# Layer 0's y tiles in three long runs between inner products, instead of eight short ones

## The chip, the cores and the metric

The kernel runs on one core of one Trainium2 chip. A core has a matrix engine (TensorE, PE in the profile, with its weight loads as PEld), a vector engine (VectorE, DVE), an activation engine (ScalarE, ACT), a general engine (GpSimd, POOL) and a queue engine (SyncE, SP) that issues most of the DMAs. Each engine takes its instructions in the order of its own list, and waits on semaphores for the others. The metric is the device time of one execution, in microseconds; the value given for a kernel is the median of its runs.

## The reference

Four layers of a graph network work on `x` (8 batches x 2048 nodes x 64 features) with one adjacency matrix `adj` (2048 x 2048). Each layer adds its result to `x` and normalises over the features. The change lies in layer 0, and in the first part of layer 1:

```python
    w = jnp.einsum('nd,dkio->nkio', embedding, weight)      # d = 16, k = 3
    b = jnp.einsum('nd,do->no', embedding, bias)
    As = [jnp.eye(N, dtype=x.dtype)]
    As.append(A)
    As.append(2.0 * (A @ As[-1]) - As[-2])
    A_stack = jnp.stack(As, 0)
    x_g = jnp.einsum('knm,bmc->bnkc', A_stack, x)
    out = jnp.einsum('bnki,nkio->bno', x_g, w)
    return out + b
    ...
    x = _layernorm(x + _L0_gnn_ref(x, adj, L0_gnn_embedding, L0_gnn_weight, L0_gnn_bias), axis=-1)
    x = _layernorm(x + _L1_gnn_ref(x, 0, L1_gnn_net_params, adj), axis=-1)
```

Layer 1 multiplies by `adj` and by a 64 x 64 matrix, with a relu, twice. Layers 2 and 3 multiply by `adj` and by small matrices too. All is in float32. `T1` is `adj @ x`, and `T2` is `adj @ T1`; the kernel folds the factor 2 and the subtraction into the weights `wn`.

## The kernel before

**Products with the adjacency.** `x` and its successors lie in SBUF as `xy`: 128 nodes in the partitions, 16 node tiles, two slots, and 512 columns (8 batches x 64 features). A product with `adj` is made in `product`, by a scheme of seven products instead of eight, at two levels. The outer level cuts nodes and columns into halves, so the result has four *quarters* (node half, column half), and makes seven inner products, in the order A11, S1, A12, S2, S4, S3, A22. Each of them (`inner`) makes seven block products (`mul`, L229). A block product loads one 1 MB tile `a` of the adjacency, or of a prepared sum of its blocks, with one DMA on SyncE (`load`, L192 or L194), and makes four matmuls of 128 x 128 weights with 512 columns (L244, or L237 in other products). The tiles `a` come from a ring of four buffers, so the loads run up to four block products ahead. From layer 1 on there are three buffers more (`ring2`, opened in `to_late`), in the memory that layer 0's last stage had used.

The block products of an inner product are made in the order `pa` (block 0), `pb` (5), `pa` (1), `pb` (6), `pc` (4), `pb` (3), `pc` (7). These are three banks of PSUM in use, but the pool `p_mm` has two: `pc` gets the one that `pa` leaves, and the next `pa` gets the one that `pb` leaves. ScalarE copies `pa` to `p1` (L259), and VectorE does the rest (L207): the operand sums `t1` to `t4`, the sums `u2` and `u3`, which have to read `pb` before the next block product adds into it, and the adds that finish a block and free its bank.

**Where y comes from.** The last product of layer 0 gives T2, feature by node, in tiles `C`. `hand_over` gives each finished 128 x 512 block as a job to the *pump*: `feature0` (L811 to L848). A job fetches its tiles of `xT` and `tT` (x and T1, feature by node) with two DMAs on SyncE, one job ahead, from two buffers each. It then has four node tiles, with two y tiles each: six matmuls in pairs, each pair being one call on the lower and one on the upper 64 rows (L829), into 128 x 1024 values. VectorE adds the first y tile into `xy`, weighted with the embedding, in eight instructions (L837). ScalarE weights the second in eight (L841), and GpSimd sums these in a tree and adds them to `xy` (L846, L848). A job has 48 matmul calls. There are sixteen jobs, four to a quarter.

After each pair of neighbouring jobs follows a layer norm (`layernorm`, L375 on), put off by `defer` for four steps of the pump: its square on GpSimd (L396, one buffer), then, four steps later, VectorE's reduction (L402, kept in program order), small operations, ScalarE's square root (L407) and the scaling (L412). A quarter has two of them.

**What sets the order.** The program's order is that of the pump: after every block product, `mul` calls `pump.step(rate)`, and `step` takes the number of steps from the first job, when `batch` steps are owed. With `rate=4` and `batch=16` that is sixteen steps, two jobs of 96 matmul calls in all, after every four block products. Steps that have no job count half for deferred norms. `pass_mark` at the start of the next product takes all jobs up to the mark (set after S4, so the quarters (0,0) and (0,1)), and `flush(False)` takes the norms that the next product needs. The quarters come in the order (0,0), (0,1), (1,1), (1,0). A scheduler then orders the instructions of each engine by priority as far as dependencies, buffers and `keep_in_program_order` allow it: so single y matmuls that need only x can be moved ahead, into earlier inner products.

In layer 1, `product` is called with the first two inner products, A11 and S1, ahead of `pump.drain()`, which ends layer 0's jobs, and of `to_late`, which gives back its pools.

Of the kernel before, what the change touches and what calls it, by code (L numbers as in the profile page):

```python
# [29 lines left out]
class Pump:  # L30


    def __init__(self):
        self.jobs = []
        self.later = []
        self.rate = 1
        self.gate = None
        self.owed = 0
        self.batch = 1

    def add(self, gen):
        self.jobs.append(gen)
# [22 lines left out]
    def tick(self, idle=False):  # L65
        for job in list(self.later):

            job[0] -= 0.5 if idle and job[4] else 1
            if job[0] <= 0:
                job[0], job[4] = job[1], False  # L70
                if next(job[2], "done") == "done":
                    self.later.remove(job)

    def step(self, n=1, now=False):
        self.owed += n
        if self.jobs and self.owed < self.batch and not now:
            return
        n, self.owed = int(self.owed), self.owed - int(self.owed)
        while n > 0 and (self.jobs or self.later):
            try:  # L80
                idle = not self.jobs
                if not idle:
                    next(self.jobs[0])
                n -= 1
                self.tick(idle)
            except StopIteration:
                self.jobs.pop(0)
# [8 lines left out]
def kernel(  # L96
# [18 lines left out]
    nc = tc.nc  # L115
# [7 lines left out]
    NP = B // 2  # L123
# [70 lines left out]
            nc.sync.dma_start(a, comb[q][s].rearrange("p (n m c) -> p n m c", n=TG, m=TG))  # L194
        return a

    def product(src, feature, between=None, rate=1, own=None, pin=False, batch=1, onto_slot=None):

# [9 lines left out]
        def new_t():  # L210
            return sums.tile([P, NT // 2, 4 * F], F32, tag="T", name="T", bufs=3)
# [4 lines left out]
        def inner(q, b, finish, early=None):  # L216


            b11, b12, b21, b22 = (
                b[:, hm * TG : (hm + 1) * TG, ts(hc, 2 * F)] for hm in range(2) for hc in range(2)  # L220
            )

            def new():
                return sums.tile([P, TG, 2 * F], F32, tag="t", name="t", bufs=5)

            t1 = add(new(), b12, b11, ALU.subtract)
            t2 = add(new(), b22, t1, ALU.subtract)
            t3 = add(new(), b22, b12, ALU.subtract)
            t4 = add(new(), b21, t2, ALU.subtract)  # L229

            def mul(ps, s, xb, start, stop=True):
                a = load(q, s)
                if onto_slot is not None:

                    for k in range(TG):
                        for m in range(TG):
                            nc.tensor.matmul(  # L237
                                ps[:, ts(k, P)], a[:, k, m, :], xb[:, m, :],
                                start=(start and k == m == 0), stop=(m == TG - 1), skip_group_check=True,
                            )  # L240
                    pump.step(pump.rate)
                    return
                for m in range(TG):
                    nc.tensor.matmul(  # L244
                        ps, xb[:, m, :], a[:, :, m, :], start=(start and m == 0),
                        stop=(m == TG - 1), skip_group_check=True,
                    )
                pump.step(pump.rate)

            def bank(n):  # L250
                nonlocal banks
                banks += 1
                pool = p_mm if p_mm2 is None or banks % 3 else p_mm2
                return pool.tile([P, GW], F32, tag="mm", name=f"mm{n}")

            pa, pb = bank("a"), bank("b")
            mul(pa, 0, b11, True)
            p1 = sums.tile([P, GW], F32, tag="p1", name="p1")
            nc.scalar.copy(p1, pa)  # L259
            if early is not None:  # L260
                early(2, p1)
            mul(pb, 5, t2, True)
            u2 = add(sums.tile([P, GW], F32, tag="u2", name="u2"), pb, p1)
            if early is not None:
                early(1, u2)
            mul(pa, 1, b21, False)
            finish(0, pa, None)
            mul(pb, 6, t3, False)
            u3 = add(sums.tile([P, GW], F32, tag="u3", name="u3"), pb, p1)
            if early is not None:  # L270
                early(3, u3)
            pc = bank("c")
            mul(pc, 4, t1, True)
            finish(3, pc, u3)
            mul(pb, 3, t4, False)
            finish(2, pb, p1)
            mul(pc, 7, b22, False)
            finish(1, pc, u2)

        def fresh(c):  # L280
            def finish(blk, ps, plus):
                if plus is None:
                    nc.scalar.copy(c[:, blk, :], ps)
                else:
                    add(c[:, blk, :], ps, plus)
            return finish,
# [42 lines left out]
        if pin:  # L329
            tc.keep_in_program_order(sub)  # L330
        inner(A11, b11, *fresh(u))
        inner(S1, t1, *fresh(v))
        pump.drain()
        pump.rate, pump.batch = rate, batch
        if between is not None:
            between()
        t2 = new_t()
# [3 lines left out]
        prior(0, 0)  # L341
        c = new_c()
        inner(A12, b21, *onto(c, u, (0, 0)))
        t3 = new_t()
        sub = nc.vector.tensor_tensor(t3, b22, b12, ALU.subtract)
        if pin:
# [3 lines left out]
        prior(1, 0)  # L350
        c = new_c()
        inner(S2, t2, *onto(u, u, then=lambda blk: add(c[:, blk], u[:, blk], v[:, blk])))
        inner(S4, b22, *onto(c, c, (0, 1)))
        pump.mark()
        prior(1, 1)

# [4 lines left out]
            hand_over(v, 1, 1, blk)  # L361

        inner(S3, t3, *onto(u, u, then=last))
        inner(A22, t4, *onto(u, u, (1, 0)))

    def to_nodes(dst, pool, tiles, p, hT):
# [72 lines left out]
    if True:  # L439
# [353 lines left out]
        if True:  # L793
            p_y = first.enter_context(tc.tile_pool(name="p_y", bufs=3, space=PSUM))
            l0y = first.enter_context(tc.tile_pool(name="l0y", bufs=1))
            e_sb = l0y.tile([P, NT, D], F32, tag="e_sb", name="e_sb")
            nc.gpsimd.dma_start(e_sb, emb)


            order = [  # L800
                (2 * ih + k // 2, 2 * ch + k % 2)
                for ih, ch in ((0, 0), (0, 1), (1, 1), (1, 0)) for k in DONE
            ]
            fetched = {}

            def fetch(k):
                if k < len(order):
                    i, p = order[k]
                    fetched[i, p] = [l0y.tile([P, GW], F32, tag=n, name=n, bufs=2) for n in ("xT", "tT")]
                    for tile_, src in zip(fetched[i, p], (xT, t1T)):  # L810
                        nc.sync.dma_start(tile_, src[p][:, ts(i, GW)])  # L811

            def feature0(g, p, hT):
                if (g, p) == order[0]:
                    fetch(0)
                fetch(order.index((g, p)) + 1)
                terms = fetched.pop((g, p)) + [hT]
                for k in range(TG):
                    t = g * TG + k
                    acc = xy[:, t, 0, ts(p, 2 * F)].rearrange("p (b f) -> p b f", f=F)  # L820


                    s = l0y.tile([P, DH, 2, F], F32, tag="s", name="s", bufs=2)
                    for h in range(2):
                        y = p_y.tile([P, 2, DH * F], F32, tag="y", name="y")
                        for n in range(3):
                            for b in range(2):
                                half = slice(b * F, (b + 1) * F)
                                nc.tensor.matmul(  # L829
                                    y[:, b, :], terms[n][half, ts(k, P)],  # L830
                                    wn[half, n, h * DH : (h + 1) * DH, :],
                                    start=(n == 0), stop=(n == 2),
                                )
                        for d in range(DH):
                            e = e_sb[:, t, h * DH + d : h * DH + d + 1]
                            if h == 0:
                                nc.vector.scalar_tensor_tensor(  # L837
                                    acc, y[:, :, ts(d, F)], e, acc, ALU.mult, ALU.add
                                )
                            else:  # L840
                                nc.scalar.activation(s[:, d], y[:, :, ts(d, F)], AF.Copy, scale=e)  # L841
                        if h == 0:
                            yield
                    n = DH // 2
                    while n:
                        nc.gpsimd.tensor_tensor(s[:, :n], s[:, :n], s[:, n : 2 * n], ALU.add)  # L846
                        n //= 2
                    nc.gpsimd.tensor_tensor(acc, acc, s[:, 0], ALU.add)  # L848
                    yield

            product(1, then(feature0, 0, gap=4, pool_sq=True), rate=4, batch=16)


    late = p_z = None
# [127 lines left out]
```

## Time and profile before

| what | value |
|---|---|
| median of three runs | 1682.71 us (1682.04 to 1684.85) |
| the profiled execution, its own time | 1684.56 us |
| its span, first to last instruction | 1682.8 us |
| mean granted clock of TensorE | 0.997 |
| instructions in the profile | 20633 |
| HBM read and written | 339.85 MB, 50.33 MB |
| y matmuls (L829), union of their time | about 395 us (133.1 + 131.3 + 131.2) |
| first and last y matmul | 220.7 and 744.0 us from the span's start |

The profile is that of one execution. *Busy* is the time in which at least one instruction of an engine was running. TensorE's matmuls overlap, and their ends are modelled, so distances between starts say more than durations. A row of the timeline gives the start, the time to the end of the last instruction that it merges, engine, line of the kernel, operation, output and inputs, their shape, and the number merged; in brackets stands the idle time ahead of it and what is taken to have ended it. Where several semaphores are waited for, that is the one that came last by the profile, and not always the true one.

### The profile page before, as it was taken

The numbers are of one execution on the slowest core, as the hardware profiler recorded it, in microseconds if no ns is written. First come the engines' busy times: TensorE is split into PE (matmuls) and PEld (weight loads), VectorE is DVE, ScalarE is ACT, GpSimd is POOL, SyncE is SP. The second block draws the span as 40 slices with busy tenths as digits, with TensorE's granted clock in tenths as the row PEclk, the third lists the DMA queues.
The fourth block names the chain that finished last, engine by engine and source line by source line (L and its number), as shares of the span: only waits on it lengthen the run. The fifth ranks groups of instructions, "written<-read, shape, count | busy, mean of one in ns | idle before, by whom it ended". The sixth has DMA issues, their size and how long they took to land.

```text
span 1682.8 us, 20633 instructions
## 1 busy us (share of the span) xinstructions
PE 1666.6 (99%) x8176; PEld 1045.7 (62%) x8176; DVE 946.1 (56%) x1690; ACT 265.9 (16%) x763; POOL 250.3 (15%) x332
## 2 busy tenths in 40 slices
PE   9999999999999999999999999999999999999997
PEld 4688844444444444444454455589998455579997
DVE  5587893555546556454533365863568344543666
ACT  0100000421332332330011011220001011100001
POOL 1121200542435544450000000000000000000000
PEclk9999999999999999999999999999999999999999
DMA  9998888135233223309877877657888866678894
GB/s 341 351 359 309 306 312 305 42 113 189 87 125 113 68 71 126 113 34 366 307 268 269 307 252 262 224 209 273 293 292 299 305 217 230 230 266 296 315 311 155
DMA packets 82288, 391.53 MB, mean 233 GB/s; under 512 B 8880, under 2 KB 25264, under 8 KB 42640
## 3 DMA queue, kind: packets, MB, share of 16 engines
q1 hardware_dynamic: 69504, 346.78, 58.3%
q0 software_dynamic: 11248, 42.08, 6.5%
q10 hardware_dynamic: 1440, 1.35, 0.3%
q8 instruction: 65, 1.06, 0.2%
q14 instruction: 31, 0.25, 0.0%
HBM read 339.85 MB, written 50.33 MB: 232 GB/s over the span
## 4 chain that ended last, share of the span: by engine, by line
PE 96%; DVE 3%; POOL 0%; ACT 0%; issue 0%; POOLq 0%; DVEq 0%; ACTq 0%
PE y L829 20%; PE mmb L244 17%; PE mmc L244 11%; PE mma L244 11%; PE ps_n L689 9%; PE mmb L237 8%; PE mmc L237 6%; PE mma L237 6%; PE ps_n L652 3%; PE z L877 2%; PE z L906 2%; PE pt L868 1%; DVE ss L402 0%; PE pt_n L370 0%; DVE xy L412 0%; DVE sm L386 0%
## 5 line engine op out<-in xcount | busy, mean ns | idle before, releaser
L244 PE MATMUL mmb<-a,t 128*128 128x512 f32 x672 | 303.6, 593 | 1.2 <-DVE xy L412 1.2
L837 DVE SCALAR_TENSOR_TENSOR xy<-y,e_sb,xy 128x128 f32<-128x128 f32 x512 | 179.6, 351 | 137.5 <-PE y L829 121.6
L244 PEld LDWEIGHTS mmb<-a,t 128*128 128x128 f32 x672 | 125.8, 190 | 153.9 <-issue 151.0
L846 POOL TENSOR_TENSOR s<-s 128x512 f32<-128x512 f32 (+2 forms) x192 | 159.1, 828 | 333.6 <-ACT s L841 323.5
L841 ACT ACTIVATE s<-y,e_sb 128x128 f32<-128x128 f32 x512 | 139.2, 383 | 270.1 <-PE y L829 270.1
L207 DVE TENSOR_TENSOR u<-mmb,p 128x512 f32<-128x512 f32 x84 | 57.9, 689 | 189.8 <-PE mmb L244 135.2
L237 PE MATMUL mmb<-t,a 128*128 128x128 f32 x1344 | 157.1, 275 | 0.0
L237 PEld LDWEIGHTS mmb<-t,a 128*128 128x128 f32 x1344 | 153.5, 192 | 0.0
L829 PE MATMUL y<-wn,xT 64*128 64x512 f32 x512 | 133.1, 592 | 0.0
L829 PE MATMUL y<-wn,tT 64*128 64x512 f32 x512 | 131.3, 589 | 0.0
L829 PE MATMUL y<-wn,C 64*128 64x512 f32 x512 | 131.2, 589 | 0.0
L244 PE MATMUL mma<-a,T 128*128 128x512 f32 x256 | 115.6, 594 | 0.0
L244 PE MATMUL mmc<-a,t 128*128 128x512 f32 x224 | 101.2, 595 | 0.0
L244 PE MATMUL mma<-a,xy 128*128 128x512 f32 x192 | 88.8, 604 | 2.2 <-DVE C L207 2.2
L829 PEld LDWEIGHTS y<-wn,xT 64*128 64x128 f32 x512 | 49.2, 187 | 63.3 <-issue 62.9
L829 PEld LDWEIGHTS y<-wn,tT 64*128 64x128 f32 x512 | 49.5, 187 | 60.6 <-issue 60.6
L829 PEld LDWEIGHTS y<-wn,C 64*128 64x128 f32 x512 | 49.6, 187 | 60.3 <-issue 60.3
L259 ACT COPY p<-mma 128x512 f32<-128x512 f32 x42 | 24.5, 584 | 390.5 <-PE mma L244 256.3
L244 PEld LDWEIGHTS mma<-a,T 128*128 128x128 f32 x256 | 47.6, 190 | 56.9 <-issue 56.5
L207 DVE TENSOR_TENSOR C<-mmc,C 128x512 f32<-128x512 f32 x48 | 33.1, 690 | 88.3 <-PE mmc L244 78.9
L244 PEld LDWEIGHTS mmc<-a,t 128*128 128x128 f32 x224 | 41.3, 190 | 47.8 <-issue 47.4
L244 PEld LDWEIGHTS mma<-a,xy 128*128 128x128 f32 x192 | 36.4, 193 | 47.3 <-issue 42.2
(127 smaller groups left out, 2055.8 us busy)
## 6 DMA issues: line engine op xcount, KB each, us to landing
a<-comb SPq DMA_DIRECT2D x240, 1024.0 KB, 4.8
a<-in_blocks SPq DMA_DIRECT2D x54, 1024.0 KB, 4.9
comb<-si POOLq DMA_DIRECT2D x28, 1024.0 KB, 10.6
a<-in_slices SPq DMA_DIRECT2D x15, 1024.0 KB, 9.4
comb<-so POOLq DMA_DIRECT2D x16, 512.0 KB, 6.9
comb<-so POOLq DMA_DIRECT2D x16, 256.0 KB, 8.5
t1T<-hT SPq DMA_DIRECT2D x16, 256.0 KB, 4.3
xT<-in_xT SPq DMA_DIRECT2D x16, 256.0 KB, 3.2
```

The lines of the kernel that those rows point to most:

```text
L207: nc.vector.tensor_tensor(out, a, b, op)
L237: nc.tensor.matmul(ps[:, ts(k, P)], a[:, k, m, :], xb[:, m, :], start=(start and k == m == 0), stop=(m == TG - 1), skip_group_check=True,)
L244: nc.tensor.matmul(ps, xb[:, m, :], a[:, :, m, :], start=(start and m == 0), stop=(m == TG - 1), skip_group_check=True,)
L259: nc.scalar.copy(p1, pa)
L652: mm = nc.tensor.matmul(ps[p], xcol(0, TG * j + m, p), ch[j][:, m], start=(n == 0 and m == 0), stop=(n == NG - 1 and m == TG - 1), skip_gr ...
L689: nc.tensor.matmul(ps[:, ts(p, GW // 2)], b(k, p), a(k // TG, k % TG), start=(start and p == k == 0), stop=(k == NT // 2 - 1), skip_group_ ...
L829: nc.tensor.matmul(y[:, b, :], terms[n][half, ts(k, P)], wn[half, n, h * DH : (h + 1) * DH, :], start=(n == 0), stop=(n == 2),)
L837: nc.vector.scalar_tensor_tensor(acc, y[:, :, ts(d, F)], e, acc, ALU.mult, ALU.add)
L841: nc.scalar.activation(s[:, d], y[:, :, ts(d, F)], AF.Copy, scale=e)
L846: nc.gpsimd.tensor_tensor(s[:, :n], s[:, :n], s[:, n : 2 * n], ALU.add)
L877: nc.tensor.matmul(z[:, k, :], aT[:, ts(k, P)], wd[:, w, :], start=(n == 0), stop=(n == len(terms) - 1),)
L906: nc.tensor.matmul(z[n][:, k], xT[half, ts(k, P)], w[half], start=True, stop=True)
```

## The change

The pump gets a `hold` instead of a `batch`: while it holds and there are jobs, `step` does nothing at all. A new method `run(n)` takes the next `n` jobs (or all) in one go. `product` gets `runs`, which says after which inner product how many jobs are run: four after S2 and four after S3. The other eight (quarters (1,1) and (1,0)) are left for the next product, where they run between its A11 and its S1; after that the pump no longer holds. The first matmul of every node tile is kept in program order. The number and kind of operations stay as they are.

```diff
     def step(self, n=1, now=False):
+        if self.jobs and self.hold and not now:
+            return
         self.owed += n
-        if self.jobs and self.owed < self.batch and not now:
-            return
...
+    def run(self, n=None):
+        while self.jobs and n != 0:
+            for _ in self.jobs[0]:
+                self.tick()
+            self.jobs.pop(0)
+            n = None if n is None else n - 1
...
         inner(A11, b11, *fresh(u))
+        if pump.hold:
+            pump.run()
+            pump.hold = False
         inner(S1, t1, *fresh(v))
         pump.drain()
-        pump.rate, pump.batch = rate, batch
+        pump.rate, pump.hold = rate, runs is not None
+        runs = runs or {}
...
         inner(A12, b21, *onto(c, u, (0, 0)))
+        pump.run(runs.get(A12, 0))
...
         inner(S2, t2, *onto(u, u, then=lambda blk: add(c[:, blk], u[:, blk], v[:, blk])))
+        pump.run(runs.get(S2, 0))
         inner(S4, b22, *onto(c, c, (0, 1)))
+        pump.run(runs.get(S4, 0))
         pump.mark()
...
         inner(S3, t3, *onto(u, u, then=last))
+        pump.run(runs.get(S3, 0))
         inner(A22, t4, *onto(u, u, (1, 0)))
...
-                                nc.tensor.matmul(
+                                mm = nc.tensor.matmul(
                                     y[:, b, :], terms[n][half, ts(k, P)],
...
+                                if n == b == h == 0:
+                                    tc.keep_in_program_order(mm)
...
-            product(1, then(feature0, 0, gap=4, pool_sq=True), rate=4, batch=16)
+            RUNS = {S2: NP, S3: NP}
+            product(1, then(feature0, 0, gap=4, pool_sq=True), rate=4, runs=RUNS)
```

`NP` is 4.

More of the change, by code (lines that the diff above doesn't have):

```diff
@@ L38, in __init__ @@
         self.owed = 0
-        self.batch = 1
+        self.hold = False
     def add(self, gen):
@@ L195, in load, with product @@
         return a
-    def product(src, feature, between=None, rate=1, own=None, pin=False, batch=1, onto_slot=None):
+    def product(src, feature, between=None, rate=1, own=None, pin=False, runs=None, onto_slot=None):
         def quarter(h, c):
```

## The prediction

> **What bounds the kernel now.** I read the page first, for which engine sets the end.
>
> ```profile
> PE 1666.6 (99%) x8176; PEld 1045.7 (62%) x8176; DVE 946.1 (56%) x1690; ACT 265.9 (16%) x763; POOL 250.3 (15%) x332
> ...
> PE 96%; DVE 3%; POOL 0%; ACT 0%; issue 0%; POOLq 0%; DVEq 0%; ACTq 0%
> ```
>
> TensorE is busy 99% of the span and is 96% of the chain that ended last. No matmul is added or removed here, so the change can only win or lose in the roughly 1% between and within TensorE's streams: waits, half-clock time, switches between two kinds of matmul. Next, the waits of TensorE over the whole span; the two that lie inside the layer concerned:
>
> ```profile
> PE mma L244 <- DVE C L207: 2.2, 1, 2.2
> ...
> PE mmb L244 <- DVE xy L412: 1.2, 1, 1.2
> ```
>
> Then the timeline of TensorE around the first one, with the end of the second y run (L829) in front:
>
> ```profile
> 386.80 1.02 PE L829 MATMUL y<-wn,C 64*128 64x512 f32 x4
> 387.76 3.70 PE L244 MATMUL mmc<-a,t 128*128 128x512 f32 x8
> 391.29 3.60 PE L244 MATMUL mmb<-a,t 128*128 128x512 f32 x8
> 394.73 3.60 PE L244 MATMUL mmc<-a,T 128*128 128x512 f32 x8
> 400.49 5.40 PE L244 MATMUL mma<-a,xy 128*128 128x512 f32 x8 [2.16 <-DVE C L207]
> 405.72 3.60 PE L244 MATMUL mmb<-a,t 128*128 128x512 f32 x8
> ```
>
> The first column is the start. A matmul call is two records, a block product (`mul`, four calls) eight, a pair of y calls (one to each half of the rows) four. Undisturbed starts of block products are 3.435 us apart (391.29 to 394.73), of y pairs 0.858 us. I measure everything by starts, since a matmul's end is modelled. Three excesses show. (a) Each switch: 386.80 + 0.858 = 387.66, the next starts at 387.76, and the one after is late by another 0.10. The same two tenths stand at each run's entry (342.83 + 3.435 = 346.265, y at 346.36; second y pair 0.96 later instead of 0.86). So one run of y costs 0.40 us in switches, and there are eight. (b) 394.73 to 400.49 is 5.76, which is 2.33 too much. (c) 400.49 to 405.72 is 5.23, 1.80 too much, without any wait. The granted clock explains (c); columns are the stretch, its length, TensorE's busy time and records, its clock, DMA share, GB/s:
>
> ```profile
> 390.00:398.00 8.00, 8.00 (x20) 1.00 0.56 202
> 400.60:404.10 3.50, 3.50 (x5) 0.51 0.53 222
> ```
>
> So this one stall costs 2.33 + 1.80 = 4.13 us. Why it is there is in the timeline of the other engines:
>
> ```profile
> 396.24 1.90 POOL L396 TENSOR_TENSOR sq<-xy 128x1024 f32<-128x1024 f32 x1
> 398.17 1.22 DVE L402 TENSOR_REDUCE ss<-sq 128x16 f32<-128x1024 f32 x1 [2.85 <-POOL sq L396]
> 399.80 0.63 DVE L207 TENSOR_TENSOR C<-mmb,C 128x512 f32<-128x512 f32 x1
> ```
>
> The second layer norm of a quarter starts on GpSimd (L396) only when its last y tile is added up, 10.5 us after the run's end (387.66 to 398.14). VectorE's reduction (L402) waits for it at the head of its queue, and behind it stands the add that empties a bank of `p_mm` (two banks), which the fourth block product after the run needs.
>
> The other wait (1.2) looks like the layer norm too, but that add is not what this matmul reads; I took SyncE's timeline:
>
> ```profile
> 752.24 6.59 SPq L194 DMA_DIRECT2D a<-comb  x5
> ```
>
> Nothing was issued for 8 us after the last y run (end 744.38). The first of these loads goes into memory of the y stage, and waits for the last `xy L848` on GpSimd (done 752.2); the load that the fifth block product after the run reads stands behind it. Two 1 MB transfers then need until about 759.6 (their issue to landing has a median of 9.0 us in this stretch), and the product starts at 759.71 instead of 758.3: 1.40 us.
>
> [...] a gap of 2.16 us was enough here, the 1.24 us one was not. [...] The trace has three `s` adds in 3.26 us beside VectorE adds (from 392.37) and 2.60 us otherwise (from 749.08), so the 10.5 us above can move by some tenths.
>
> **The change, part by part.** Before, a run of 96 y calls (two jobs, 41.2 us) starts whenever four block products have passed: two runs to a quarter, eight in all. After, in the built order of TensorE, the runs are 192 behind S2, 192 behind S3, and 384 behind A11 of layer 1.
>
> 1. *Five runs fewer.* 5 x 0.40 = 2.0 us gained. Unhidden: TensorE is the bound.
>
> 2. *The pinned first matmul.* Before, two lone y calls sit in the layer's first inner product (220.72 and 228.83), each 1.05 us to the next start plus 0.10 at both ends. After, they are back in run 1, one pair, 0.858. But they covered waits. Behind the first, the next `mma` adds into the bank that ACT copies (220.87 + 0.59 = 221.46), so it can start at about 221.5 instead of 221.77. Behind the second, `mmb` needs VectorE's add (227.93 + 0.69 = 228.62), so it starts at 228.7 instead of 229.88. VectorE's order up to there is unchanged, and it is busy without a break. Net 229.88 - 228.7 = 1.2, less 0.858: 0.35 us gained. Ends: 0 and 1.64 (all excess gone).
>
> 3. *The stall at 398 goes.* S4 now starts straight after run 1 instead of three block products later, with both banks long empty. Let R be the start of the first block product after the run (387.76 in the trace above). VectorE's order is then first norm (ends R + 4.4), `C<-C,p`, u2 (its matmul ends R + 7.1; done 7.8; needed at 10.4), two adds, then the wait for the square (R + 10.4), reduction, two small ones, and `C<-mma,C`, done at about R + 12.7, as its counterpart at 400.43. The bank is needed by the fifth block product, at R + 13.8. Spare: 1.1 us. Gain 4.13. If the square comes 1.1 us later the wait begins; 2 us more and the clock falls too. Behind that, the second norm ends at R + 15.5 and u3 at 16.2, needed at 17.3.
>
> 4. *Run 2, then A22, then layer 1.* Ticks stop while jobs are held, so the second norm of quarter (0,1) is flushed at the start of layer 1. With E the start of A11: last add of A22 E + 0.9, norm 3.8 (744.98 to 748.74 in the trace), T of 2048 elements 2.3, one add 0.7, then u2, done at E + 8.4; needed at E + 10.3. The square is done long before. Cost 0; if the cover is gone, u2 is late next.
>
> 5. *Run 3, 384 calls, 165 us.* In the run VectorE has 3.05 us, ACT 2.18, GpSimd 2.6 + 0.46 per 5.15 us of TensorE; none accumulates. Quarter (1,1)'s two norms fall inside the run. Before, one does as well (558.39 to 562.2, inside the run from 537.08), and no y pair there is late. Cost 0.
>
> 6. *The loads after run 3.* The memory-bound load still stands ahead of the load of the fifth block product after the run (now all five are of S1), and waits for the same GpSimd tail. Same stall, 1.40 us: no gain.
>
> 7. *DMA.* Fetches of xT and tT (two per job) now queue eight together in SyncE's order, each waiting for the job two before. The last waits for the run's end, but four loads of `a` are already in, and the fifth must wait for the first block product anyway (R + 3.6; needed R + 13.8; 4.8 to land). The longest stretch of products rises from 21 to 28 block products; 21 run from 216 to 291 at 306 GB/s without a DMA wait. Cost 0.
>
> Sum: 2.0 + 0.35 + 4.13 = 6.5 us. Profiled span 1682.8 becomes 1676.3 (that execution took 1684.56, 1.8 more than its span, and becomes 1678.1). The median of the runs shown is 1682.71; I take the same 6.5 off: 1676.2, 0.39% less. About 0.2% (3.4 us) is what a measurement of this kernel tells from no change.
>
> **Rivals.** *The stall comes back at another run's end.* VectorE is held by a norm after every run, and spare times are 1.1, 1.9 and about 1.5 us. For it: the GpSimd tail varies with VectorE. Against: the steps above are copied from this trace. Only the switches and singles remain: 2.35 us, 1680.4.
>
> *More goes than I count:* the stall after run 3 also vanishes (if the load is issued at once), and the singles' waits too: 6.5 + 1.4 + 1.3 = 9.2, 1673.5. Against it, the load's waits are the same in the built order.
>
> *Nothing noticeable:* the trace's 4.1 us stall is an accident of this execution and mostly absent in the timed runs; then 2.35 too. The timed runs spread over 2.8 us, so it can't be excluded.
>
> *Slower:* the GpSimd tail after run 3 grows. It holds SyncE's head load, and with it TensorE one for one; from a stall of 2.2 us the clock falls, 1.8 more. The present one is 1.4. If the tail comes 4.7 us later the whole gain is gone; 10 later gives 1682.7 + 5.3 = 1688. For it, only this run has eight jobs unbroken; against it, GpSimd works 3.1 of each 5.15 us and its order is unchanged.
>
> **How the numbers follow.** Forecast as summed: 70%. Stall elsewhere or accidental, together 14%. More than counted 8%. Slower 8%. The range goes down to the 9.2 us case, 1673.5, and up past 1680.4 by the 1.1 us that the first rival's new stall may last before its cover is gone wholly, 1681.5; it leaves out the slower case and little else. Faster by over 0.2% (below 1679.3): 70 + 8, and a little of the middle case: 0.79. Within: 0.13. Slower: 0.08. The likeliest case's own range is 1675 to 1678.
>
> **What would show it.** In the trace after: three y runs near 315 to 397, 445 to 528, 576 to 741; no lone y call; four switches of 0.10 at each run; no wait of TensorE on VectorE after run 1 and clock 1.00 there; the load stall of about 1.4 us still in the fifth block product after run 3. A half-clock stretch behind any run, a wait on `C L207` at R + 13.8, or a late u2 at the layer's boundary would make me wrong.

## The result, and the profile after

| | before | after |
|---|---|---|
| median | 1682.43 us (12 runs, 1681.67 to 1684.85) | 1678.78 us (12 runs, 1677.79 to 1681.21) |
| profiled execution, its own time | 1684.56 us | 1678.49 us |
| its span | 1682.8 us | 1676.7 us |
| mean granted clock | 0.997 | 0.998 |
| A11 of the second product to layer 1's first `z` matmul | 570.94 us | 565.09 us |

The ratio is 0.9979, with a 95% interval of 0.9972 to 0.9987: 0.21% less, or 3.65 us between the medians, where 6.5 us had been forecast. From one profile to the other it is 6.1 us in the span. The last row is taken from TensorE's timeline: from the start of the first block product of the second product (216.31 us before, 215.70 after) to the first matmul that writes `z` in layer 1 (787.25 and 780.79). Everything that the change touches lies in between. I call it the stage, and compare profiles by it; what lies ahead of it starts up to 2.1 us earlier or later from one execution to the next, and behind it the distances are the same to 0.03 us (207.68 us to the first `pt` transpose, 675.6 from there to the last block product).

The stage became 5.85 us shorter. First the page of the kernel after, the line of busy times:

```profile
PE 1660.1 (99%) x8176; PEld 1046.1 (62%) x8176; DVE 945.1 (56%) x1690; ACT 265.1 (16%) x763; POOL 246.0 (15%) x332
```

The same 8176 matmuls are there, and TensorE is busy 6.5 us less: part of what it lost before was counted as busy (half clock, and the modelled ends). From its waits, those that lie in the stage (us in total, times, longest):

```profile
PE mmc L253 <- DMA a<-comb: 1.9, 1, 1.9
...
PE mma L253 <- DMA t1T<-hT: 0.7, 1, 0.7
```

The wait of 2.2 us on `C L207` is gone. A wait on a load is there, longer than the one that stood in the same place before (1.24 us), and a new small one in A11 (0.7).

The timeline of TensorE at the end of the first run (`y`, now L846; products are L253):

```profile
395.73 1.02 PE L846 MATMUL y<-wn,C 64*128 64x512 f32 x4
396.69 3.70 PE L253 MATMUL mma<-a,xy 128*128 128x512 f32 x8
400.23 3.60 PE L253 MATMUL mmb<-a,t 128*128 128x512 f32 x8
403.66 3.60 PE L253 MATMUL mma<-a,xy 128*128 128x512 f32 x8
407.09 3.60 PE L253 MATMUL mmb<-a,t 128*128 128x512 f32 x8
410.53 3.60 PE L253 MATMUL mmc<-a,t 128*128 128x512 f32 x8
```

From 400.23 on, every start is 3.43 or 3.44 us after the one before: no wait and no half clock (the granted clock of this profile is 1.00 from 4.97 to 1670.67 us). The two switches show as 396.69 - 395.73 = 0.96 and 400.23 - 396.69 = 3.54, a tenth each too long. The runs go from 314.09 to 396.6, 444.95 to 527.5 and 575.82 to 740.7. What had caused the stall is still there, on GpSimd and VectorE, but falls behind another bank:

```profile
404.83 2.22 POOL L413 TENSOR_TENSOR sq<-xy 128x1024 f32<-128x1024 f32 x1
...
407.52 1.21 DVE L419 TENSOR_REDUCE ss<-sq 128x16 f32<-128x1024 f32 x1
...
409.14 0.63 DVE L216 TENSOR_TENSOR C<-mma,C 128x512 f32<-128x512 f32 x1
```

The add that frees the bank ends at 409.77; the block product that needs it, the fifth behind the run, was due at 410.53 and started in its turn. The spare time is 0.76 us.

Behind the third run stands the load stall. The lines are from the timelines of TensorE, SyncE and GpSimd; in brackets stands the wait:

```profile
751.22 3.60 PE L253 MATMUL mmb<-a,t 128*128 128x512 f32 x8
756.68 3.67 PE L253 MATMUL mmc<-a,t 128*128 128x512 f32 x8 [1.86 <-DMA a<-comb]
```

```profile
748.58 3.16 SPq L202 DMA_DIRECT2D a<-comb  x4
```

```profile
748.10 0.45 POOL L867 TENSOR_TENSOR xy<-xy,s 128x128 f32<-128x128 f32 x1
```

As in the kernel before, SyncE issues nothing until GpSimd's last add is done (748.55), 7.8 us after the run's end (740.82). The product then starts 5.46 us after the one before instead of 3.435: 2.03 us too late, where the kernel before had 1.40. So the stage adds up as 2.0 for five runs fewer, 0.36 in A11, 4.13 for the stall before S4, less 0.63 for the longer load wait: 5.86, measured 5.85. The 0.36 is the time by which A11 became shorter, from its start to its fifth block product (233.42 - 216.31 = 17.11 before, 231.59 - 215.70 = 15.89 after), less the 0.86 of the y pair that now stands in run 1.

Why the medians show only 3.65 us is in the times of the runs. Those of the kernel before, 41 of them in the largest set, fall into two groups: 33 between 1681.7 and 1683.1 us, and 8 between 1684.1 and 1684.9. Those after do too: 8 between 1677.8 and 1679.1, and 4 between 1680.0 and 1681.2. The profiled execution of before (1684.56) was one of the slower group, that of after (1678.49) one of the faster. The mean granted clock on record for each execution goes with the groups: after, it is 0.997 in all four of the slower group and 0.998 or 0.999 in the other eight; before, it is 0.997 in six of the eight, 0.998 in two, and 0.998 or 0.999 in the 33. The other two sets of the kernel before have 2 slow ones of 12 and 3 of 22. The last experiments below show what tells the groups apart.

### The profile page after: what moved, and what is told of

It reads as the page before. It is cut to its first block, busy times and chain, and to the rows that moved or that the text cites. A ratio compares the mean times of both kernels' runs of the same rounds, so it can differ in the third digit from the quotient of the medians.

```text
span 1676.7 us, 20632 instructions
## 1 busy us (share of the span) xinstructions
PE 1660.1 (99%) x8176; PEld 1046.1 (62%) x8176; DVE 945.1 (56%) x1690; ACT 265.1 (16%) x763; POOL 246.0 (15%) x332
## 4 chain that ended last, share of the span: by engine, by line
PE 95%; DVE 3%; DMA 1%; ACT 0%; POOL 0%; issue 0%; SPq 0%; POOLq 0%; ACTq 0%
PE y L846 20%; PE mmb L253 17%; PE mmc L253 12%; PE mma L253 11%; PE ps_n L706 9%; PE mmb L246 8%; PE mmc L246 6%; PE mma L246 6%; PE ps_n L669 3%; PE z L898 2%; PE z L927 2%; PE pt L889 1%; DMA a<-comb 0%; DVE ss L419 0%; DMA xy<-in_x 0%; PE pt_n L387 0%
## 5 line engine op out<-in xcount | busy, mean ns | idle before, releaser
L253 PE MATMUL mmb<-a,t 128*128 128x512 f32 x672 | 303.4, 593 | 0.0
L253 PEld LDWEIGHTS mmb<-a,t 128*128 128x128 f32 x672 | 126.3, 190 | 151.6 <-issue 149.2
L846 PE MATMUL y<-wn,xT 64*128 64x512 f32 x512 | 131.6, 591 | 0.0
L846 PE MATMUL y<-wn,tT 64*128 64x512 f32 x512 | 131.2, 589 | 0.0
L846 PE MATMUL y<-wn,C 64*128 64x512 f32 x512 | 131.2, 589 | 0.0
L253 PE MATMUL mma<-a,T 128*128 128x512 f32 x256 | 115.6, 595 | 0.0
L253 PE MATMUL mmc<-a,t 128*128 128x512 f32 x224 | 101.1, 594 | 1.9 <-DMA a<-comb 1.9
L253 PE MATMUL mma<-a,xy 128*128 128x512 f32 x192 | 87.0, 594 | 0.7 <-DMA t1T<-hT 0.7
L846 PEld LDWEIGHTS y<-wn,xT 64*128 64x128 f32 x512 | 49.3, 187 | 61.1 <-issue 60.7
L846 PEld LDWEIGHTS y<-wn,tT 64*128 64x128 f32 x512 | 49.7, 187 | 60.2 <-issue 60.2
L846 PEld LDWEIGHTS y<-wn,C 64*128 64x128 f32 x512 | 49.7, 187 | 60.2 <-issue 60.2
L253 PEld LDWEIGHTS mma<-a,T 128*128 128x128 f32 x256 | 47.7, 190 | 56.8 <-issue 56.5
L253 PEld LDWEIGHTS mmc<-a,t 128*128 128x128 f32 x224 | 41.5, 190 | 49.3 <-issue 48.7
L706 PE MATMUL ps_n<-a,xy 128*128 128x256 f32 x288 | 64.4, 380 | 0.0
## 6 DMA issues: line engine op xcount, KB each, us to landing
comb<-si POOLq DMA_DIRECT2D x28, 1024.0 KB, 10.5
```

The source lines that it names most:

```text
L253: nc.tensor.matmul(ps, xb[:, m, :], a[:, :, m, :], start=(start and m == 0), stop=(m == TG - 1), skip_group_check=True,)
L706: nc.tensor.matmul(ps[:, ts(p, GW // 2)], b(k, p), a(k // TG, k % TG), start=(start and p == k == 0), stop=(k == NT // 2 - 1), skip_group_ ...
L846: mm = nc.tensor.matmul(y[:, b, :], terms[n][half, ts(k, P)], wn[half, n, h * DH : (h + 1) * DH, :], start=(n == 0), stop=(n == 2),)
```

## The experiments

Each edit is to the kernel before or to the kernel after, as said. The median of the kernel before, beside them, was 1682.29 us (41 runs) for the first four, 1682.22 us (22 runs) for the next three, and 1682.74 us (one run) for the last three, which have a single time each.

**The stall's cause: the norms later.** In the kernel before, the reduction of a norm follows its square after 16 steps of the pump instead of 4.

```diff
-                    pump.defer(norm, gap, need=i < NG // 2)
+                    pump.defer(norm, gap, 16, need=i < NG // 2)
```

> The kernel before, with the second half of each deferred norm put off by 16 steps of the pump instead of 4, so that the reduction that waits for GpSimd no longer stands ahead of the add that frees the bank behind the second y run. My theory: the stall before S4 (2.33 us, and 1.80 us of half clock) goes from the trace, and nothing else moves by more than some tenths; span 1678.7 us. If the half clock comes with this stall in every execution, the median falls by 4.1 us to 1678.3; if it comes in only some of them, as the timed runs of before suggest (two of twelve near 1684.5, the rest near 1682.2), by 2.3 us to 1680.1. Rival (the stall has another cause than the norm): 1682.4, with the stall still there.

Measured: 1680.72 us (13 runs, 1680.28 to 1682.65), ratio 0.9990 (0.9981 to 0.9998); stage 567.32 us, 3.62 less. TensorE's timeline at the place of the stall, in this kernel:

```profile
389.18 3.70 PE L244 MATMUL mmc<-a,t 128*128 128x512 f32 x8
392.72 3.60 PE L244 MATMUL mmb<-a,t 128*128 128x512 f32 x8
396.15 3.60 PE L244 MATMUL mmc<-a,T 128*128 128x512 f32 x8
399.59 3.60 PE L244 MATMUL mma<-a,xy 128*128 128x512 f32 x8
```

The eight runs, the banks and the place of S4 are as before; only the norms moved, and the stall of 4.13 us is gone. So it was VectorE, held at the head of its queue: in the profile of before it idled 2.85 us ahead of the norm's reduction (L402, started at 398.17), and the add that frees the bank ran behind that, at 399.80. The expectation that nothing else would move by more than some tenths failed: the rest of the difference comes from two other places. The load wait behind the last run vanished (1.40), since ScalarE's share of the last job no longer stands behind the norm's square root (5.02 us idle ahead of it, up to 746.72, in the profile of before) and SyncE's loads start 5.6 us after the run instead of 7.8. And two new waits stand within y runs, where a late norm holds VectorE when it should free a bank of `y`:

```profile
572.25 1.02 PE L829 MATMUL y<-wn,C 64*128 64x512 f32 x4
573.99 1.13 PE L829 MATMUL y<-wn,xT 64*128 64x512 f32 x4 [0.72 <-DVE xy L837]
```

The next start is 1.74 us later instead of 0.86; twice, 1.77 in all. Sum: -4.13 - 1.40 + 1.77 = -3.76, measured -3.62. The median fell by 1.57 us, not by 3.6, since most executions of the kernel before (33 of 41) are in the faster group, and the one profiled of that group (1682.38 us, below) has no half clock. The slowest execution, 1682.65 us, is the one profiled: its clock is 0.999, and its stage only began late (217.74), so a long time alone does not show half clock.

**The pin alone.** The kernel before, with the change's pin of each node tile's first matmul and nothing else.

```diff
-                                nc.tensor.matmul(
+                                mm = nc.tensor.matmul(
...
+                                if n == b == h == 0:
+                                    tc.keep_in_program_order(mm)
```

> The kernel before with the first y matmul of each node tile kept in program order, and nothing else of the change. My theory: the two lone y calls in A11 go back into the first run, the waits that they covered come up, and 0.35 us are gained (1682.1 us); the stall before S4 stays. Rival: they covered nothing, 1.6 us are gained (1680.8 us).

Measured: 1684.04 us (13 runs), ratio 1.0001 (0.9993 to 1.0009); stage 570.57 us, 0.37 less. TensorE's timeline in A11:

```profile
221.43 1.12 PE L244 MATMUL mma<-a,xy 128*128 128x512 f32 x2 [0.72 <-ACT p L259]
222.39 3.60 PE L244 MATMUL mmb<-a,t 128*128 128x512 f32 x8
225.83 2.74 PE L244 MATMUL mma<-a,xy 128*128 128x512 f32 x6
228.59 3.70 PE L244 MATMUL mmb<-a,t 128*128 128x512 f32 x8
```

The y singles that stood there are gone, and the wait for ScalarE's copy that they had covered takes the first one's place (0.72), so the net is the forecast 0.37. The times tell another thing. The median is 1.75 us above that of the kernel before although the stage is shorter: 8 of 13 executions lie between 1683.95 and 1684.25, and 5 between 1681.6 and 1682.3. The slower group, all eight at a clock of 0.997, grew from about one in five to eight in thirteen, with the same stall (2.2 us on `C L207`) unchanged before S4.

**Twice as many runs.** The kernel before with one job at a time, so sixteen runs.

```diff
-            product(1, then(feature0, 0, gap=4, pool_sq=True), rate=4, batch=16)
+            product(1, then(feature0, 0, gap=4, pool_sq=True), rate=4, batch=8)
```

> The kernel before with a run of one job (48 y calls) after every two block products, sixteen runs instead of eight. My theory: eight more runs at 0.40 us of switches each cost 3.2 us, 1685.6 us, if no stall comes or goes with the new order; in the trace each run shows 0.10 us at entry, 0.10 behind its first pair, 0.10 at exit and 0.10 behind the first block product. Rival (a switch costs nothing outside of modelled ends, and the change's gain is all in the stall): 1682.4 us.

Measured: 1684.23 us (21 runs, 1683.65 to 1686.9), ratio 1.0012 (1.0005 to 1.0018); stage 571.14 us, 0.20 more. A run's entry in its timeline (products L244, y L829):

```profile
332.91 3.70 PE L244 MATMUL mma<-a,T 128*128 128x512 f32 x8
336.44 3.60 PE L244 MATMUL mmb<-a,t 128*128 128x512 f32 x8
339.97 1.13 PE L829 MATMUL y<-wn,xT 64*128 64x512 f32 x4
340.93 1.02 PE L829 MATMUL y<-wn,tT 64*128 64x512 f32 x4
...
756.53 3.70 PE L244 MATMUL mma<-a,T 128*128 128x512 f32 x8 [1.67 <-ACT p L259]
```

The first product after a run takes 3.53 us to the next start, the second 3.53 to the run's entry, and the first y pair 0.96: a tenth four times, as everywhere. Eight runs more cost 3.2 us. That only 0.20 shows is because the stall before S4 went here too (4.13; with runs of one job the norms fall behind other block products), while the wait in layer 1's S1 grew by 0.43 (last line) and a y pair waits for 0.57: 3.2 - 4.13 + 0.43 + 0.57 = 0.07. The two terms can't be told apart by this time alone; the timeline tells them. Held against the kernel before without half clock (the execution of 1682.38 us below, stage 569.17, load wait 1.32) the stage is 1.97 us longer, and the sum 3.2 - 2.33 + 0.51 + 0.57 = 1.95; the medians are 1.94 apart.

**The load out of its place.** The kernel after, with SyncE's three loads into the new buffers in the y stage's memory (the fifth to seventh counted from `to_late`) kept in program order, so that the loads of layer 1's S1 no longer stand behind them.

```diff
-            nc.sync.dma_start(a, blocks[i + s // 2, j + s % 2])
+            dma = nc.sync.dma_start(a, blocks[i + s // 2, j + s % 2])
...
+        if ring2 is not None and RING < loads <= RING + 3:
+            tc.keep_in_program_order(dma)
```

> The changed kernel, with the first loads into the memory of the y stage kept in program order on SyncE, so that they no longer stand ahead of the loads of layer 1's S1. My theory: the load of the fifth block product after the last run is issued when its buffer comes free, about 4 us earlier, the wait of 1.9 us in layer 1's S1 goes, and with it the half clock that it brings in some executions; 1676.6 us median, and a spread of under 1.5 us. Rival (the wait is on the layer norm, as the waits of the kernel before have it): 1678.8 us.

Measured: 1676.53 us (5 runs, 1676.43 to 1677.3), ratio to before 0.9966 (0.9953 to 0.9978); stage 562.98 us, 2.11 less than after. SyncE and TensorE behind the third run:

```profile
745.38 7.19 SPq L202 DMA_DIRECT2D a<-comb  x3
```

```profile
752.05 3.60 PE L255 MATMUL mmb<-a,t 128*128 128x512 f32 x8
755.49 3.60 PE L255 MATMUL mmc<-a,t 128*128 128x512 f32 x8
```

The first load goes 3.7 us after the run's end (741.65) instead of 7.8, and the fifth block product starts 3.44 us after the fourth. The wait is gone, and none of the five executions stands apart as slower. This version's median is 2.25 us below the changed kernel's and 5.8 us below the kernel's before.

**The same in the kernel before.** The pin of the loads alone, on the kernel before.

> The kernel before with the same loads kept in order. Its wait of 1.24 us in layer 1's S1 is put down to the layer norm on VectorE. My theory: it is the load, and goes; 569.5 us from the first block product to the first projection instead of 570.94, the wait before S4 stays, 1680.9 us median. Rival (it is the norm): 570.9, 1682.3 us.

Measured: 1680.97 us (12 runs, 1680.39 to 1683.19), ratio 0.9993 (0.9984 to 1.0001); stage 569.37 us, 1.57 less. In its waits, and at the fifth block product behind the last run:

```profile
PE mma L246 <- DVE C L209: 2.1, 1, 2.1
```

```profile
754.92 3.60 PE L246 MATMUL mma<-a,T 128*128 128x512 f32 x8
758.36 3.60 PE L246 MATMUL mmb<-a,t 128*128 128x512 f32 x8
```

The stall before S4 stays, and the 1.24 us that the profile of before puts down to the norm (`xy L412`) is gone, though the norm stands where it stood. It was the load, as the prediction had read it. The waits and the timeline show this; the ratio alone, with 1.0 within its interval, would not.

**Two runs instead of three.** The kernel after, with eight jobs behind S3, none behind S2, and then the same with the loads pinned.

```diff
-            RUNS = {S2: NP, S3: NP}
+            RUNS = {S3: 2 * NP}
```

> The changed kernel with two y runs of eight jobs instead of three: all of the first eight after S3, the other eight where they are. My theory (0.40 us of switches to a run, and nothing else at stake): from the first block product of layer 0's second product to the first projection of layer 1 0.4 us less than in the changed kernel (564.7 against 565.09 us), the load wait in layer 1's S1 as it is; median 1678.4 us. Rival (a longer run leaves VectorE and GpSimd further behind): a new wait of TensorE behind the first run, 1680 us or more.

> Both together: two runs, and the loads into the memory of the y stage kept in order. My theory: the gains add up; 562.6 us from the first block product to the first projection (565.09 - 2.1 - 0.4), median 1676.1 us, below all others. Rival (the two share a cause): no less than the kernel with the pinned loads alone, 1676.5 us.

Measured: 1678.97 us (10 runs, 1677.81 to 1681.43), ratio to before 0.9980 (0.9971 to 0.9989), so no different from after; with the loads pinned 1676.49 us (5 runs, 1676.17 to 1677.06), ratio 0.9963 (0.9951 to 0.9976), no different from three runs with the loads pinned, the stage 0.28 us longer. The 0.40 us of one run fewer is spent again. VectorE and TensorE in the first of the two:

```profile
468.80 1.22 DVE L429 TENSOR_TENSOR xy<-xy,rs 128x1024 f32<-128x1024 f32 x1
470.06 0.69 DVE L216 TENSOR_TENSOR t<-xy 128x512 f32<-128x512 f32 x1
```

```profile
472.43 1.02 PE L846 MATMUL y<-wn,C 64*128 64x512 f32 x4
473.86 1.13 PE L846 MATMUL y<-wn,xT 64*128 64x512 f32 x4 [0.40 <-DVE xy L856]
```

The norms within run 3 of the kernel after made no y pair late: TensorE has no gap there. Here the scheduler put an operand sum `t` right behind a norm, ahead of VectorE's part of y, and the y pair came 0.57 us late. In the profile without the pin the load wait was 2.24 us with half clock behind it (0.60 over 757.60:761.00, next start 5.21 us later), so its stage (567.44) can't be held against the 565.09 of after; it is 0.17 us above the 567.27 of after's second profile (below), which has half clock in the same place.

**What the two groups of times are.** The kernels before and after once more, unchanged, each with a profile of its own; before twice.

> The kernel before, unchanged, profiled once more, to see an execution without half clock behind the stall before S4. Theory: the wait of TensorE on the bank's add is itself a little shorter where the clock stays up: the executions with and without half clock lie 2.66 us apart (1684.76 and 1682.1), 0.86 more than the 1.80 us of the half clock, so the wait would be about 1.3 to 1.6 us instead of 2.16. Rival: the wait is the same 2.1 to 2.2 us and only the clock differs; then the executions should lie 1.8 us apart, and the rest of the 2.66 comes from elsewhere in the program. A time near 1682 is expected with either; if it is near 1684.7, the half clock is there again and the run tells nothing on this.

> The kernel before, unchanged, a third profile, for the same question. Theory: wait of 1.3 to 1.6 us, next block product 3.43 us later (no half clock), stage from A11 of the second product to layer 1's first z about 568.3 us. Rival: wait of 2.1 to 2.2 us and no half clock, stage about 569.1 us.

> The changed kernel, unchanged, profiled once more. The run ends and S4 should show no wait again (spare 0.66 us in the first profile). The load wait in layer 1's S1 was 1.86 us, 0.6 more than in the kernel before; if that is the transfer's own spread, it can lie anywhere from 1.2 to 2.2 us here, and half clock follows only near the upper end (then a time of 1680 to 1681 instead of 1678.5). If it is the change's doing, it is 1.8 to 1.9 us again.

Measured: 1686.0, 1682.38 and 1680.85 us. The stall of the kernel before, first in the execution of 1686.0, then in that of 1682.38 us (TensorE's timeline, S4's first two block products):

```profile
401.90 5.40 PE L244 MATMUL mma<-a,xy 128*128 128x512 f32 x8 [2.15 <-DVE C L207]
407.13 3.60 PE L244 MATMUL mmb<-a,t 128*128 128x512 f32 x8
```

```profile
400.07 3.70 PE L244 MATMUL mma<-a,xy 128*128 128x512 f32 x8 [2.16 <-DVE C L207]
403.61 3.60 PE L244 MATMUL mmb<-a,t 128*128 128x512 f32 x8
```

The wait is the same, 2.15 and 2.16 us. In the one the next product starts 5.23 us later, in the other 3.54. So the theory that the wait is shorter where the clock stays up fell, and the rival holds: the same wait is followed by half clock in some executions and not in others. The stages are 570.92 and 569.17 us, 1.75 apart; the 1686.0 is longer still because its stage began 1.4 us later than in the first profile of before.

The place of the wait among the changes of the clock differs. In the first profile of before the granted clock rises to 1.00 at 8.15 us into the span, falls to 0.50 at 400.68, rises at 404.09 and falls again at 1677.26, behind the last matmul. The later three lie 115.0, 116.0 and 489.0 times 3.4133 us after the first rise. In the first profile of after it rises at 4.97 and falls at 1670.67, 488.0 times 3.4133 us later. So I cut the traces into stretches of this length, from the first rise on. They lie differently on the program in each execution: the stage began 208.16 us after the first rise in that profile of before, 210.73 in that of after, and 208.96 in the one of 1682.38 us (first rise at 6.94). TensorE in two neighbouring stretches, first in the profile of 1684.56 us, then in that of 1682.38 (stretch, its length, busy time and records, clock, DMA share, GB/s):

```profile
397.27:400.68 3.41, 1.25 (x4) 1.00 0.92 312
400.68:404.09 3.41, 3.41 (x5) 0.50 0.50 211
```

```profile
396.07:399.48 3.41, 1.84 (x5) 1.00 0.81 293
399.48:402.89 3.41, 2.82 (x7) 1.00 0.71 293
```

In the first the whole wait of 2.16 us lies in one stretch, and half clock fills the next. In the second a stretch ends in the middle of the wait, so it is cut into 1.57 and 0.59 us, and the clock stays at 1.00. Of the 488 whole stretches between the first rise and TensorE's last matmul in the first profile of before, the one with 2.16 us of idle time is the only one that half clock follows; the others have 1.08 us at most. Of the 487 in the first of after none has more than 1.08 us, and half clock follows none. That the place of the wait decides is my reading of these profiles; what sets the clock is not shown.

The kernel after had this time, in the timelines of TensorE and SyncE:

```profile
751.39 3.60 PE L253 MATMUL mmb<-a,t 128*128 128x512 f32 x8
757.34 5.37 PE L253 MATMUL mmc<-a,t 128*128 128x512 f32 x8 [2.36 <-DMA a<-comb]
762.55 3.60 PE L253 MATMUL mmb<-a,t 128*128 128x512 f32 x8
```

```profile
748.75 3.16 SPq L202 DMA_DIRECT2D a<-comb  x4
```

The end of run 1 is undisturbed again. The load wait is 2.36 us, with half clock behind it (762.55 - 757.34 = 5.21), and the stage 567.27. Its issue is again 7.8 us after the run's end (740.98), but the product starts 8.59 us after the issue. In the three profiles with eight jobs in the last run (after twice, and two runs) this distance is 8.10, 8.59 and 8.48 us; in the kernel before, three times, 7.47, 7.46 and 7.39. So the longer wait came with the changed order in each of its three profiles. In slices of half a microsecond the DMA's rate climbs within 2 us to about 420 GB/s in both, so the start is not what differs; in the first profiles, the sixteen parts of the transfer that the product waits for landed 1.17 us apart (755.38 to 756.55) after and 0.40 us apart (759.17 to 759.57) before. One part makes the difference. Fifteen had landed 7.32 to 7.37 us after the first issue in the three profiles with the longer wait, as all sixteen had 7.26 to 7.33 us after it in the three of before; the last came 0.65, 1.08 and 0.97 us behind them. In these three profiles an 8 KB packet of the profile's `instruction` queue moved within 2.2 us of the first issue (at 749.48, 750.93 and 750.06); in the three of before none did until the product had started. That this packet held the one part back is not shown, and one that came later (at 757.65 in the profile of 1682.38) had no such lag behind it.

With these two the comparison is made between like executions. Without half clock in either: stage 569.17 to 565.09, 4.08 less. With half clock in both: 570.92 to 567.27, 3.65 less.

## Why the prediction was right, and where it was not

The direction, the size within the range, and the order of events were as forecast; the likeliest case's own range (1675 to 1678) was missed by 0.8 us, for a reason that two terms of the sum show. The gain in the median is 3.65 us instead of 6.5. None of the prediction's cases gives that: it lies between the full sum and the 2.35 us of the case without the stall. That the range held is partly luck, since its width was chosen for other events.

1. *Five runs fewer, 2.0 us.* Right. Each run's four tenths stand at all three runs after, and eight runs more cost 3.2 us.
2. *The pinned first matmul, 0.35 us.* Right: 0.37, measured alone. The wait that the single had covered came back as said (after, the profile puts its 0.7 us down to `t1T`, but ScalarE's copy ended at 220.84 and the product started at 220.90).
3. *The stall before S4 goes, 4.13 us.* The mechanism is right: moving the norms alone removed it, and after the change it stayed away in both profiles, with 0.76 us of spare time instead of 1.1. The prediction has the norm's square start 10.5 us after the run; that is when it ended (398.14), and it started 8.6 us after (396.24). The sum used the end, so it stands. The reduction went at R + 10.8, 0.4 later than worked out, because an add of 2.38 us on VectorE (`C<-C,u`, 405.23 on) stood ahead of it. The size was wrong for the median. Of the 4.13 us, 2.33 are in every execution profiled, and 1.80 are the half clock, which by the groups of times came in 8 of 41. The forecast summed the profiled execution and took the same sum off the median, although that execution lay 1.85 us above the median, about the price of its half clock. In the usual execution this step is worth 2.33 us.
4. *Run 2 and the boundary of layer 1.* Right: no wait there.
5. *Norms within run 3.* Right: no y pair late. Two runs, and the later norms, showed how little it takes (0.57 to 0.88 us) when something else stands beside the norm.
6. *The loads after run 3, "same stall, 1.40 us: no gain".* The stall is in the forecast place, on the forecast load, released by the same tail 7.8 us after the run. But it grew to 2.03 us and 2.52 us (756.68 - 751.22 and 757.34 - 751.39, less 3.435), since one part of the transfer landed 0.65 to 1.08 us behind the others. Behind the wait of 2.36 us the next product started 5.21 us later, at half clock; behind that of 1.86 us, 3.51. 4 of 12 executions after are in the slower group, and the one profiled of that kind has the half clock here.
7. *DMA elsewhere, 0.* Right: no other wait on a load came up in the stage.

Put together for executions without half clock: 2.0 + 0.37 + 2.33 - 0.7 (2.03 less 1.32 in the profile of 1682.38 us) = 4.0, against 4.08 in the stage. The medians of the faster groups alone, 1682.15 (10 runs) and 1678.59 (8 runs), are 3.56 apart; where the other half microsecond lies is not shown, since each stage is that of one execution. The rival that called the stall "an accident of this execution" had 1680.4 from 2.35 us; it was right about the half clock and wrong about the wait. The slower rival, a longer tail on GpSimd, did not occur: the tail ends 7.7 us after the run in both kernels. The wait for the load grew all the same, by another way. The prediction has the clock fall from a stall of about 2.2 us on. Half clock followed one of 2.16 us in the first profile of before, for 3.41 us (5.23 - 3.435 = 1.8 lost), and did not follow the one of 2.16 us in the profile of 1682.38: the length of the wait alone did not tell.

## What to carry to other kernels

Before a sum from one profile is taken off a median, compare the profiled execution's own time with the median, and say which of its terms are not in every execution: here 1.8 us of 6.5 were not. When a wait is removed, look for the next one along the same chain and price it too: a load that headed SyncE's queue but went into memory still in use held back the loads behind it until 7.8 us after the run's end, and keeping the needed ones in order was worth more (2.1 us of stage, 2.25 in the median) than another run fewer (nothing). Costs of this kind don't add: one run fewer, a later norm or a pin each moved work under another wait, so each was worth measuring alone.

## What the runs showed of the hardware

- *The same wait was followed by half clock in some executions and not in others.* Behind a TensorE wait of 2.15 or 2.16 us the next start came 5.16 to 5.24 us later in four profiles of the kernel before and its variants (1684.56, 1686.0, 1684.14 with the pin alone, and 1683.15 with the load pinned), and 3.54 us later in a fifth (1682.38). Behind waits of 2.24 and 2.36 us it came 5.21 us later in both, behind waits of 1.67 and 1.86 us 3.54 and 3.51 us later.
- *In two profiles the clock's changes lay whole multiples of 3.4133 us behind its first rise:* 115.0, 116.0 and 489.0 in the first of before, 488.0 in the first of after. Of stretches of that length, one with 2.16 us of idle time was followed by half clock, and one with 1.57 us (in the profile of 1682.38) was not. What holds between these two is not shown.
- *How often it came* is known from the groups of times alone: 8 of 41 executions, but 8 of 13 when the pin had made the way to the stall 0.4 us shorter. Why is not shown.
- *What it cost:* 3.41 us at a clock of 0.50 in the first profile of before (400.68 to 404.09). In the six profiles that have it the product behind the wait took 5.16 to 5.24 us to the next start, instead of 3.44.
- *One part of sixteen held up a transfer:* it landed 0.65 to 1.08 us behind the other fifteen in three profiles, and 0.04 to 0.08 us behind them in three others, at the same rate of some 420 GB/s.
- *An add of VectorE took longer while GpSimd squared:* in the stage of the first profile of after, `C<-C,u` took 2.38 us twice, at 405.23 and 536.09, both begun while GpSimd squared (404.83 to 407.05, 535.69 to 537.91), and 0.68 to 0.69 us the other nine times, with no GpSimd work beside it.
